# Two more table parts held, a shared tile for them and a pair of places, one uF tile, another cut of the last part, splits further ahead in two chunks

## The chip, the cores and the metric

One core of a Trainium2 chip runs the kernel. The metric is the device time of one execution in microseconds (us), from start to end. Durations of single instructions and transfers come from a profiled execution of the same program.

## The reference

The inputs are a table of 100,001 rows of 128 floats, 1024 sequences of 50 item numbers, and 1024 lengths. The reference gathers the rows, takes prefix means over the 50 steps, normalises each step over the batch, runs a spiking recurrence over the 50 steps, and multiplies the spike rates by the whole table:

```python
emb = emb_table.at[0].set(0.0)
e = emb[seq]                                   # 1024 x 50 x 128
uF = cumsum(e, axis=1) / minimum(t, lengths)   # prefix means
y = (uF - uF.mean(0)) * rsqrt(uF.var(0) + 1e-5) * gamma + beta
def step(v, x):
    v = v + (x - v) / 2.0
    spike = (v >= 1.0)
    return v - spike, spike
scores = spikes.mean(axis=0) @ emb.T           # 1024 x 100001, float32
```

The scores are 409.6 MB, and the table is 51.2 MB.

## The kernel before

**Two stages.** The first runs 50 steps. GpSimd (POOL) gathers eight times 128 table rows a step (`gather`, L196), TensorE (PE) transposes and accumulates them (L309, L270), VectorE (DVE) and ScalarE (ACT) do the statistics and the recurrence (L318 to L366). The second, from about 580 us on, computes the scores: counts (spike counts, 8 blocks of 128 batch rows) times the table.

**Parts, pairs, places.** The table is cut into 98 parts of 1024 rows; the last has 673. A part lies in SBUF as 128 partitions x 4 KB. `prepare` splits a part: eight PE transposes (L124) into a PSUM tile `pt`, an ACT copy that rounds to `hi` (L146), a DVE subtraction for the rest, `lo` (L147). A pair (hi, lo) needs a free place of 8 KB per partition; the list `free` hands places out first in, first out. `product` makes two matmuls for each 512 columns, so four per part and block (L154). Four PSUM tiles of 1024 columns serve products and transposes in turn.

**Chunks and blocks.** `WIDTHS` cuts the 98 parts into chunks: four of 2 parts (c = 0 to 3), four of 3 (c = 4 to 7), thirteen of 6 (c = 8 to 20). Within a chunk, n runs over the 8 batch blocks. A block (c, n) multiplies its parts, evicts them from PSUM into an output tile `o`, by DVE (L483) and ACT (L485) in turn, and stores the tile with one DMA on SP's queue (L163): 1 MB, 1.5 MB or 3 MB. `ready` issues one split after blocks n = 2 to 6, and one behind each part of block n = 7, if a place is free and the limit q2 (the end of the next chunk) isn't reached. The program order of each engine is the order in which this is written (`manual_schedule`).

**Where the parts come from.** 38 parts (`held`) are loaded on SP's queue in the first stage: six groups of six, and, when parts 0 and 1 have been split at t = 42 and 44, two more in their places. The other 60 come on ACT's queue in the second stage, three at a time, at n = 1 and 4 of the chunks from c = 8 on. The last of these loads takes two whole parts, the 673 rows' 640 first as 128 x 5 pieces of 512 B (L111), and 33 single rows (L116).

**Output tiles and where they lie.** Pools are laid out in the order in which they are opened, tiles within a pool in the order in which their tags are first used. Phase-one pools (`once`, ..., `uF`, `gather`) and later the pool `o` begin at the same address, behind the rows. In bytes per partition from that address:

| chunks | in the pool `o` | order of output tiles |
|---|---|---|
| 0 to 3 | third pair 0 to 8192; o0 from 8192, o1 from 16384, o2 from 24576, o3 from 32768, 8 KB each | o0, o1, o2, o3 |
| 4 to 7 | o2 from 0, o0 from 12288, o1 from 24576, 12 KB each | o2, o0, o1 |
| 8 to 20 | two pairs 0 to 16384; o 16384 to 40960 | the rows' tile 2, the rows' tile 3, o |

Chunks 4 to 7 have 32 blocks, so block (7, 5) uses o1, (7, 6) o2 and (7, 7) o0. The first two 1024-column results of block (0, 0) go out through single 4 KB tiles: one in a gather buffer, one in the second `uF` buffer, 23200 bytes from the start of the pool `once`. In that pool `rlen` lies at 7584 to 11680. A tile that is laid over older ones waits for the readers of each tile that it overlaps.

**Semaphores of the transfers.** The trace names a semaphore for each DMA. Those of SP's and ACT's queues together take eight of them in turn, and each issue first waits on the semaphore that it is going to use.

Of the kernel before, what the change touches and what calls it, by code (L numbers as in the profile page):

```python
# [12 lines left out]
F32 = mybir.dt.float32  # L13
BF16 = mybir.dt.bfloat16
F32R = mybir.dt.float32r
# [5 lines left out]
P = 128  # L21
BN_EPS = 1e-5
V_TH = 1.0
HALF = 1024
KQ = HALF // P
BANK = 512
GROUP = 6
AHEAD = 6
ONLY = 5
TWICE = 2  # L30

WIDTHS = 4 * [2] + 4 * [3] + 13 * [6]
NARROW, MIDDLE = 4, 8
# [3 lines left out]
def rec_kernel(  # L37
# [9 lines left out]
    nc = tc.nc  # L47
    B, T = seq.shape
    N, D = table.shape
    NB = B // P  # L50
# [8 lines left out]


    rowp = ctx.enter_context(tc.tile_pool(name="rows", bufs=1))


    countA = const.tile([P, P], F32R, tag="countA", name="countA")
# [5 lines left out]
    ident = const.tile([P, P], F32, tag="ident", name="ident")  # L70
# [2 lines left out]

    parts = -(-N // HALF)
    assert sum(WIDTHS) == parts
    held = AHEAD * GROUP + TWICE
    rows = {}
    split = {}

    free = []  # L80
# [4 lines left out]
    def size(q):  # L85
        return min(HALF, N - q * HALF)

    def group(g):
        at = g if g < AHEAD else AHEAD - 2 + g % 2
        r = rowp.tile([P, GROUP, HALF], F32, tag=f"rows{at}", name=f"rows_{g}")  # L90
        for k in range(GROUP):
            rows[g * GROUP + (TWICE if g else 0) + k] = r[:, k, :]
        return r

    def fetch(r, q, n):

        engine = nc.sync if q < held else nc.scalar
        k = q if q < GROUP else (q - TWICE) % GROUP
        n = min(n, parts - q)
        whole = n - (size(q + n - 1) < HALF)  # L100
        if whole:
            engine.dma_start(
                out=r[:, k : k + whole, :],
                in_=table[q * HALF : (q + whole) * HALF, :].rearrange("(q p k) d -> p q (k d)", p=P, k=KQ),
            )
        if whole < n:
            full, rest = divmod(size(parts - 1), P)
            c1 = (parts - 1) * HALF
            r = r[:, k + whole, :].rearrange("p (k d) -> p k d", d=D)
            if full:  # L110
                engine.dma_start(  # L111
                    out=r[:, :full, :],
                    in_=table[c1 : c1 + full * P, :].rearrange("(k p) d -> p k d", p=P),
                )
            if rest:
                engine.dma_start(out=r[:rest, full, :], in_=table[c1 + full * P : N, :])  # L116

    def turned(q, pt):
        r = rows.pop(q)
        if q == 0:  # L120
            nc.vector.memset(r[0:1, :D], 0.0)
        for k0 in range(0, size(q), P):
            kw = min(P, size(q) - k0)
            nc.tensor.transpose(pt[:, k0 : k0 + kw], r[:kw, k0 : k0 + D], ident[:kw, :kw])  # L124

    def views(q, pt, hi, lo):
        hw = size(q)
        if hw < HALF:
            return pt[:, :hw], hi[:, :hw], lo[:, :hw]
        return (  # L130
            pt.rearrange("d (k p) -> d p k", k=KQ),
            hi.rearrange("d (p k) -> d p k", k=KQ),
            lo.rearrange("d (p k) -> d p k", k=KQ),
        )


# [1 line left out]
    def prepare(q, pt):  # L138
        turned(q, pt)
        split[q] = hi, lo = free.pop(0)  # L140
        hw = size(q)
        if hw % 2:
            nc.vector.memset(hi[:, hw : hw + 1].bitcast(F32), 0.0)
            nc.vector.memset(lo[:, hw : hw + 1].bitcast(F32), 0.0)
        vp, vh, vl = views(q, pt, hi, lo)
        nc.scalar.copy(vh, vp)  # L146
        nc.vector.tensor_tensor(vl, vp, vh.bitcast(F32), ALU.subtract)  # L147
# [18 lines left out]
    with ExitStack() as ph:  # L166
        once = ph.enter_context(tc.tile_pool(name="once", bufs=1))
        lp = ph.enter_context(tc.tile_pool(name="lif", bufs=1))
        sp = ph.enter_context(tc.tile_pool(name="stats", bufs=3))
        up = ph.enter_context(tc.tile_pool(name="uF", bufs=2))  # L170
        gp = ph.enter_context(tc.tile_pool(name="gather", bufs=2))
        accp = ph.enter_context(tc.tile_pool(name="acc", bufs=1, space=bass.MemoryType.PSUM))
        vp = ph.enter_context(tc.tile_pool(name="v", bufs=1, space=bass.MemoryType.PSUM))
# [8 lines left out]
        nc.sync.dma_start(out=gb[:, 0:1], in_=gamma.rearrange("(d o) -> d o", o=1))  # L182
        nc.sync.dma_start(out=gb[:, 1:2], in_=beta.rearrange("(d o) -> d o", o=1))
        first = group(0)
        fetch(first, 0, GROUP)
        for g in range(1, AHEAD):
            fetch(group(g), g * GROUP + TWICE, GROUP)

# [42 lines left out]
        rlen = once.tile([P, B], F32, tag="rlen", name="rlen")  # L233
# [57 lines left out]
        whole = slice(0, B)  # L291
# [6 lines left out]
        for t in range(T):  # L298
            last = t == T - 1
            e = es.pop(t)  # L300
# [4 lines left out]
            uF = up.tile([P, B], F32, tag="uF", name=f"uF_{t}")  # L305
# [26 lines left out]
            r = sp.tile([P, 1], F32, tag="r", name=f"r_{t}")  # L332
# [14 lines left out]
            q = sp.tile([P, 1], F32, tag="q", name=f"q_{t}")  # L347
# [20 lines left out]
            if not last:  # L368
                vt = vp.tile([P, B], F32, tag=f"v{t % 2}", name=f"v_{t}")
                x(vt, whole)  # L370
                if t:
                    spiked(count, whole, v)
                step(vt, whole)
                v = vt
                d = over(t, v)
                if t + 2 < T:
                    l = only(t + 2)

                if t in (T - 8, T - 6):
                    q = (t - T + 8) // 2  # L380
                    pair(q)
                    prepare(q, vp.tile([P, HALF], F32, tag="v1", name=f"pt_{q}"))
                    if q == TWICE - 1:
                        for k in range(TWICE):
                            rows[GROUP + k] = first[:, k, :]
                        nc.sync.dma_start(
                            out=first[:, :TWICE, :],
                            in_=table[GROUP * HALF : (GROUP + TWICE) * HALF, :].rearrange(
                                "(q p k) d -> p q (k d)", p=P, k=KQ
                            ),  # L390
                        )
# [16 lines left out]

        po0 = accp.tile([P, HALF], F32, tag="po0", name="po_0_0")
        po1 = vp.tile([P, HALF], F32, tag="v0", name="po_0_1")  # L410
        for q, (pool, tag, po) in enumerate(((gp, "e", po0), (up, "uF", po1))):
            o = pool.tile([P, HALF], F32, tag=tag, name=f"o_0_{q}")
            for h, cs in enumerate(halves):
                product(po[:, cs], q, 0, h * BANK, BANK)
            for h, cs in enumerate(halves):
                if q and h:
                    nc.vector.tensor_scalar_mul(o[:, cs], po[:, cs], 1.0 / T)
                else:
                    nc.scalar.mul(o[:, cs], po[:, cs], 1.0 / T)
                store(0, q * HALF + h * BANK, o[:, cs])  # L420
# [10 lines left out]
    q0 = 0  # L431
    to_split = WIDTHS[0]
    to_fetch = held

    def places(at):
        t = rowp.tile([P, GROUP, HALF], F32R, tag=f"rows{at}", name=f"pairs_{at}")
# [2 lines left out]
    for c, W in enumerate(WIDTHS):  # L439

        if c in (0, NARROW, MIDDLE):
            opening.close()
            where = opening if c < MIDDLE else ctx
            op = where.enter_context(tc.tile_pool(name="o", bufs=1, reuse_waits="tile"))
            if c == 0:
                third = [op.tile([P, HALF], F32R, tag=x, name=x) for x in ("hi2", "lo2")]
                free.append(third)
                turns = [(op, f"o{k}", 2) for k in range(4)]
            elif c == NARROW:
                assert third in free  # L450
                free.remove(third)
                turns = [(op, f"o{k}", 3) for k in (2, 0, 1)]
            else:
                fourth = op.tile([P, 4, HALF], F32R, tag="pairs", name="pairs")
                free.extend((fourth[:, k, :], fourth[:, k + 1, :]) for k in (0, 2))
                turns = [(rowp, "rows2", 6), (rowp, "rows3", 6), (op, "o", 6)]
            blocks = 0
        q1 = q0 + W
        q2 = q1 + (WIDTHS[c + 1] if c + 1 < len(WIDTHS) else 0)

        def ready():
            nonlocal to_split
            if to_split < q2 and free:
                prepare(to_split, psum.tile([P, HALF], F32, tag="ps", name=f"pt_{to_split}"))
                to_split += 1

                if to_split in (GROUP + TWICE, 2 * GROUP + TWICE):
                    places(to_split // GROUP - 1)

        for n in range(NB):  # L470
            if c == 0 and n == 0:
                continue
            pool, tag, most = turns[blocks % len(turns)]
# [17 lines left out]
                    ready()  # L491
            if c or n > 1:
                store(n, q0 * HALF, o[:, : min(N, q1 * HALF) - q0 * HALF])
            if 2 <= n < NB - 1:
                ready()

            if n in (1, 4) and c >= MIDDLE and to_fetch < parts:
                g, k = divmod(to_fetch - TWICE, GROUP)
                if k or to_split >= (g - 1) * GROUP + TWICE:
                    if k == 0:  # L500
                        r = group(g)
                    fetch(r, to_fetch, GROUP // 2)
                    to_fetch += GROUP // 2
        assert to_split == q2
        q0 = q1


# [17 lines left out]
```

## Time and profile before

| what | value |
|---|---|
| median of 5 runs | 1642.88 us (1642.73 to 1648.5) |
| profiled execution, own time | 1643.19 us |
| its span, first to last instruction | 1641.1 us |
| PE / DVE / ACT / POOL busy | 1093.5 / 944.0 / 668.8 / 387.8 us |
| stores on SP's queue and the loads before them | 429.81 MB |
| loads on ACT's queue in the second stage | 31.28 MB |
| mean granted TensorE clock | 0.96 |

The page has the busy time of each engine, the span in 40 slices of 41 us (busy tenths, granted clock, DMA share, GB/s), the DMA queues, the chain of work that ended last, and the costliest groups. Other views of the trace are the waits by engine, the chain in order of time, the timeline, tables of stretches, and for each DMA the times at which its 16 shares landed. In a timeline line, the bracket says how long the engine stood idle before the instruction and what ended that.

### The profile page before, as it was taken

The numbers are of one execution on the slowest core, as the hardware profiler recorded it, in microseconds if no ns is written. First come the engines' busy times: TensorE is split into PE (matmuls) and PEld (weight loads), VectorE is DVE, ScalarE is ACT, GpSimd is POOL, SyncE is SP. The second block draws the span as 40 slices with busy tenths as digits, with TensorE's granted clock in tenths as the row PEclk, the third lists the DMA queues.
The fourth block names the chain that finished last, engine by engine and source line by source line (L and its number), as shares of the span: only waits on it lengthen the run. The fifth ranks groups of instructions, "written<-read, shape, count | busy, mean of one in ns | idle before, by whom it ended". The sixth has DMA issues, their size and how long they took to land.

```text
span 1641.1 us, 12239 instructions
## 1 busy us (share of the span) xinstructions
PE 1093.5 (67%) x4450; PEld 812.3 (50%) x4450; DVE 944.0 (58%) x1125; ACT 668.8 (41%) x697; POOL 387.8 (24%) x408
## 2 busy tenths in 40 slices
PE   4332333333333399888988788888788887888884
PEld 2111111111122276666866666666666666666763
DVE  5665665665565866566755555555545555555552
ACT  2332332332333355455544444444444444444442
POOL 7666666666766600000000000000000000000000
PEclk9999999999999999999999999899989999999998
DMA  9511111111111289999999999999999999999998
GB/s 349 209 47 45 48 47 47 45 46 46 49 48 45 64 328 416 405 424 414 405 425 427 431 431 422 419 427 421 424 430 417 419 418 415 431 427 419 398 430 342
DMA packets 51897, 488.12 MB, mean 297 GB/s; under 512 B 10075, under 2 KB 11004, under 8 KB 30588
## 3 DMA queue, kind: packets, MB, share of 16 engines
q1 hardware_dynamic: 30464, 429.81, 62.3%
q0 software_dynamic: 12800, 26.24, 5.5%
q10 hardware_dynamic: 8572, 31.28, 4.8%
q8 instruction: 35, 0.57, 0.1%
q14 instruction: 26, 0.21, 0.0%
HBM read 77.69 MB, written 409.60 MB: 297 GB/s over the span
## 4 chain that ended last, share of the span: by engine, by line
DMA 45%; POOL 13%; PE 12%; DVE 9%; issue 7%; another core or an unknown queue 7%; ACT 6%; ACTq 0%; SPq 0%; DVEq 0%; POOLq 0%
DMA scores<-o 44%; POOL e L196 13%; PE po L154 11%; ACT o L485 4%; DVE bs L319 2%; DVE uF L318 1%; DVE v L366 1%; DVE o L483 1%; DVE negv L286 1%; DMA e<-in_L_rec_emb_table,idx 1%; ACT v L363 1%; DVE count L289 1%; PE pt L124 0%; ACT pairs L146 0%
## 5 line engine op out<-in xcount | busy, mean ns | idle before, releaser
L483 DVE TENSOR_SCALAR o<-po 128x1024 f32<-128x1024 f32 x391 | 464.4, 1221 | 345.5 <-DMA scores<-o 305.1
L485 ACT ACTIVATE o<-po 128x1024 f32<-128x1024 f32 (+1 forms) x391 | 389.7, 1018 | 539.1 <-DMA scores<-o 320.1
L196 POOL DMA_INDIRECT e<-in_L_rec_emb_table,idx x400 | 382.2, 956 | 182.4 <-issue 106.6
L154 PE MATMUL po<-pairs,countB 128*128 128x512 f32 x1136 | 305.1, 414 | 60.9 <-ACT o L485 44.0
L154 PEld LDWEIGHTS po<-pairs,countB 128*128 128x128 f32 x1136 | 218.2, 197 | 123.9 <-ACT o L485 59.1
L154 PE MATMUL po<-pairs,countC 128*128 128x512 f32 x852 | 235.8, 423 | 46.6 <-ACT o L485 46.5
L270 PE MATMUL pre<-zT,ls 128*128 128x512 f32 x100 | 78.9, 791 | 270.3 <-DVE uF L318 213.4
L154 PEld LDWEIGHTS po<-pairs,countC 128*128 128x128 f32 x852 | 166.8, 202 | 92.5 <-ACT o L485 58.1
L270 PEld LDWEIGHTS pre<-zT,ls 128*128 128x128 f32 x100 | 29.2, 293 | 310.1 <-DVE uF L318 237.8
L309 PE MATMUL pre<-ident,e 128*128 128x128 f32 x400 | 127.0, 436 | 80.4 <-DMA e<-in_L_rec_emb_table,idx 54.9
L318 DVE SCALAR_TENSOR_TENSOR uF<-rlen,pre 128x512 f32<-128x512 f32 x100 | 68.0, 680 | 174.1 <-remote 156.0
L309 PEld LDWEIGHTS pre<-ident,e 128*128 128x128 f32 x400 | 80.4, 208 | 128.3 <-DMA e<-in_L_rec_emb_table,idx 84.0
L147 DVE TENSOR_TENSOR pairs<-pt,pairs 128x1024 fp32r<-128x1024 f32 x71 | 86.3, 1222 | 94.5 <-ACT pairs L146 94.3
L333 ACT ACTIVATE r<-mv,eps 128x1 f32<-128x1 f32 x50 | 14.7, 295 | 286.0 <-DVE mv L329 196.0
L124 PE MATMUL pt<-ident,rows 128*128 128x128 f32 x782 | 113.3, 293 | 8.7 <-issue 4.9
L124 PEld LDWEIGHTS pt<-ident,rows 128*128 128x128 f32 x782 | 103.1, 154 | 27.4 <-issue 13.1
L154 PE MATMUL po<-hi,countB 128*128 128x512 f32 x216 | 88.7, 411 | 18.3 <-ACT o L485 13.8
L154 PE MATMUL po<-lo,countB 128*128 128x512 f32 x216 | 86.5, 402 | 0.0
L282 ACT ACTIVATE d<-v,less 128x1024 bf16<-128x1024 f32 x49 | 54.5, 1113 | 63.5 <-DVE v L366 41.5
L154 PE MATMUL po<-hi,countC 128*128 128x512 f32 (+1 forms) x162 | 68.4, 422 | 15.1 <-ACT o L485 15.0
L146 ACT CAST pairs<-pt 128x1024 fp32r<-128x1024 f32 x71 | 71.8, 1012 | 15.8 <-PE pt L124 15.8
L154 PE MATMUL po<-pairs,countA 128*128 128x512 f32 x284 | 71.2, 394 | 8.5 <-ACT o L485 8.3
(78 smaller groups left out, 848.9 us busy)
## 6 DMA issues: line engine op xcount, KB each, us to landing
scores<-o SPq DMA_DIRECT2D x96, 3072.0 KB
scores<-o SPq DMA_DIRECT2D x32, 1536.0 KB
scores<-o SPq DMA_DIRECT2D x30, 1024.0 KB
rows<-in_L_rec_emb_table ACTq DMA_DIRECT2D x19, 1536.0 KB
scores<-o SPq DMA_DIRECT2D x8, 2896.5 KB
rows<-in_L_rec_emb_table SPq DMA_DIRECT2D x6, 3072.0 KB
e<-in_L_rec_emb_table,idx POOLq DMA_INDIRECT x400
rows<-in_L_rec_emb_table SPq DMA_DIRECT2D x1, 1024.0 KB
```

Of the source, the lines that this page charges most:

```text
L124: nc.tensor.transpose(pt[:, k0 : k0 + kw], r[:kw, k0 : k0 + D], ident[:kw, :kw])
L146: nc.scalar.copy(vh, vp)
L147: nc.vector.tensor_tensor(vl, vp, vh.bitcast(F32), ALU.subtract)
L154: nc.tensor.matmul(po[:, :kw], lhsT=counts[n], rhs=part[:, k0 : k0 + kw], start=j == 0, stop=j == 1,)
L196: nc.gpsimd.indirect_dma_start(out=es[t][:, n * P : (n + 1) * P], out_offset=None, in_=table, in_offset=bass.IndirectOffsetOnAxis(ap=idx[: ...
L270: nc.tensor.matmul(pre[h], lhsT=l, rhs=zT[:, h * BANK : (h + 1) * BANK], start=t == 0, stop=False, skip_group_check=True,)
L282: nc.scalar.activation(d, v, AF.Identity, bias=less)
L309: nc.tensor.matmul(pre[h][:, k : k + P], lhsT=e[:, h * BANK + k : h * BANK + k + P], rhs=ident, start=False, stop=last, is_transpose=True, ...
L318: nc.vector.scalar_tensor_tensor(uF[:, cs], rlen[:, cs], 1.0 / (t + 1), pre[h], ALU.max, ALU.mult)
L319: nc.vector.bn_stats(bs[:, h, :], uF[:, cs])
L483: nc.vector.tensor_scalar_mul(o[:, h0 : h0 + hw], po[:, :hw], 1.0 / T)
L485: nc.scalar.mul(o[:, h0 : h0 + hw], po[:, :hw], 1.0 / T)
```

## The change

Forty parts are held. A new pool `aside`, opened right behind the rows and before the first stage's pools, holds a tile of 8 KB with parts 2 and 3 (`spare`). Its loads come between those of parts 0, 1 and 4 to 7 of the first group. When parts 2 and 3 have been split, the tile becomes the third pair. The pool `aside` is closed before chunk 4. So the third pair is no longer in the pool `o` of chunks 0 to 3, and is not free from the start. The pool `uF` has one buffer; the second result of block (0, 0) goes through `rlen`'s place. The pools of the first stage, and the pool `o` of chunks 0 to 3, begin 8 KB further on.

The last part is laid out as the others: 84 rows of 4 KB in one DMA, and one piece of 512 B; rows 64 to 95 are first cleared by DVE. Its split takes eight transposes of 85 rows.

In chunks 5 and 6 the limit of `ready` is 1 and 2 parts higher, and in chunk 8 splits are issued from n = 0 on. The output tiles of chunks 8 to 20 come in the order o, tile 2, tile 3.

```diff
+ASIDE = 2
+SHIFT = TWICE + ASIDE
+FURTHER = {5: 1, 6: 2}
...
+    beside = ExitStack()
+    asidep = beside.enter_context(tc.tile_pool(name="aside", bufs=1))
...
-    held = AHEAD * GROUP + TWICE
+    held = AHEAD * GROUP + SHIFT
...
         if whole < n:
-            full, rest = divmod(size(parts - 1), P)
+            full, rest = divmod(size(parts - 1), KQ)
             c1 = (parts - 1) * HALF
-            r = r[:, k + whole, :].rearrange("p (k d) -> p k d", d=D)
+            r = r[:, k + whole, :]
+            if rest:
+                at = full - full % 32
+                nc.vector.memset(r[at : at + 32, :], 0.0)
+                engine.dma_start(
+                    out=r[full : full + 1, : rest * D],
+                    in_=table[c1 + full * KQ : N, :].rearrange("(o k) d -> o (k d)", o=1),
+                )
             if full:
                 engine.dma_start(
-                    out=r[:, :full, :],
-                    in_=table[c1 : c1 + full * P, :].rearrange("(k p) d -> p k d", p=P),
+                    out=r[:full, :],
+                    in_=table[c1 : c1 + full * KQ, :].rearrange("(p k) d -> p (k d)", k=KQ),
                 )
-            if rest:
-                engine.dma_start(out=r[:rest, full, :], in_=table[c1 + full * P : N, :])
...
-        up = ph.enter_context(tc.tile_pool(name="uF", bufs=2))
+        up = ph.enter_context(tc.tile_pool(name="uF", bufs=1))
...
-        fetch(first, 0, GROUP)
+        fetch(first, 0, 0, TWICE)
+        spare = asidep.tile([P, ASIDE, HALF], F32, tag="aside", name="spare")
+        for k in range(ASIDE):
+            rows[TWICE + k] = spare[:, k, :]
+        fetch(spare, 0, TWICE, ASIDE)
+        fetch(first, TWICE, SHIFT, GROUP - TWICE)
...
-        for q, (pool, tag, po) in enumerate(((gp, "e", po0), (up, "uF", po1))):
+        for q, (pool, tag, po) in enumerate(((gp, "e", po0), (once, "rlen", po1))):
...
             opening.close()
+            if c == NARROW:
+                assert third in free
+                free.remove(third)
+                beside.close()
...
-                third = [op.tile([P, HALF], F32R, tag=x, name=x) for x in ("hi2", "lo2")]
-                free.append(third)
                 turns = [(op, f"o{k}", 2) for k in range(4)]
...
-                turns = [(rowp, "rows2", 6), (rowp, "rows3", 6), (op, "o", 6)]
+                turns = [(op, "o", 6), (rowp, "rows2", 6), (rowp, "rows3", 6)]
...
-            if to_split < q2 and free:
+            if to_split < q2 + FURTHER.get(c, 0) and free:
                 prepare(...)
                 to_split += 1
-                if to_split in (GROUP + TWICE, 2 * GROUP + TWICE):
+                if to_split == SHIFT:
+                    t = asidep.tile([P, ASIDE, HALF], F32R, tag="aside", name="third")
+                    third = (t[:, 0, :], t[:, 1, :])
+                    free.append(third)
+                if to_split in (GROUP + SHIFT, 2 * GROUP + SHIFT):
                     places(to_split // GROUP - 1)
...
-            if 2 <= n < NB - 1:
+            if (2 if c != MIDDLE else 0) <= n < NB - 1:
                 ready()
```

More of the change, by code (lines that the diff above doesn't have):

```diff
@@ L86, in size, with deep @@
         return min(HALF, N - q * HALF)
+    def deep(q):
+        return -(-size(q) // KQ)
     def group(g):
@@ L91, in group, with fetch @@
         for k in range(GROUP):
-            rows[g * GROUP + (TWICE if g else 0) + k] = r[:, k, :]
+            rows[g * GROUP + SHIFT + k if g else k + ASIDE * (k >= TWICE)] = r[:, k, :]
         return r
-    def fetch(r, q, n):
+    def fetch(r, k, q, n):
         engine = nc.sync if q < held else nc.scalar
-        k = q if q < GROUP else (q - TWICE) % GROUP
         n = min(n, parts - q)
@@ L121, in turned @@
             nc.vector.memset(r[0:1, :D], 0.0)
-        for k0 in range(0, size(q), P):
-            kw = min(P, size(q) - k0)
-            nc.tensor.transpose(pt[:, k0 : k0 + kw], r[:kw, k0 : k0 + D], ident[:kw, :kw])
+        pw = deep(q)
+        for k0 in range(0, HALF, P):
+            nc.tensor.transpose(pt[:, k0 : k0 + pw], r[:pw, k0 : k0 + D], ident[:pw, :pw])
     def views(q, pt, hi, lo):
-        hw = size(q)
-        if hw < HALF:
-            return pt[:, :hw], hi[:, :hw], lo[:, :hw]
+        pw = deep(q)
         return (
-            pt.rearrange("d (k p) -> d p k", k=KQ),
-            hi.rearrange("d (p k) -> d p k", k=KQ),
-            lo.rearrange("d (p k) -> d p k", k=KQ),
+            pt.rearrange("d (k p) -> d p k", k=KQ)[:, :pw, :],
+            hi[:, : pw * KQ].rearrange("d (p k) -> d p k", k=KQ),
+            lo[:, : pw * KQ].rearrange("d (p k) -> d p k", k=KQ),
         )
@@ L140, in prepare @@
         split[q] = hi, lo = free.pop(0)
[L141 to L144, printed above, removed]
         vp, vh, vl = views(q, pt, hi, lo)
@@ L184, in rec_kernel @@
         first = group(0)
-        fetch(first, 0, GROUP)
+        fetch(first, 0, 0, TWICE)
[4 more added lines that the diff above has]
+        fetch(first, TWICE, SHIFT, GROUP - TWICE)
         for g in range(1, AHEAD):
-            fetch(group(g), g * GROUP + TWICE, GROUP)
+            fetch(group(g), 0, g * GROUP + SHIFT, GROUP)
         es = {}
@@ L384, in rec_kernel @@
                         for k in range(TWICE):
-                            rows[GROUP + k] = first[:, k, :]
+                            rows[GROUP + ASIDE + k] = first[:, k, :]
                         nc.sync.dma_start(
                             out=first[:, :TWICE, :],
-                            in_=table[GROUP * HALF : (GROUP + TWICE) * HALF, :].rearrange(
+                            in_=table[(GROUP + ASIDE) * HALF : (GROUP + SHIFT) * HALF, :].rearrange(
                                 "(q p k) d -> p q (k d)", p=P, k=KQ
@@ L433, in rec_kernel @@
     to_fetch = held
+    third = None
     def places(at):
@@ L445, in rec_kernel @@
             if c == 0:
-                third = [op.tile([P, HALF], F32R, tag=x, name=x) for x in ("hi2", "lo2")]
-                free.append(third)
                 turns = [(op, f"o{k}", 2) for k in range(4)]
             elif c == NARROW:
-                assert third in free
-                free.remove(third)
                 turns = [(op, f"o{k}", 3) for k in (2, 0, 1)]
@@ L461, in ready @@
         def ready():
-            nonlocal to_split
-            if to_split < q2 and free:
+            nonlocal to_split, third
+            if to_split < q2 + FURTHER.get(c, 0) and free:
                 prepare(to_split, psum.tile([P, HALF], F32, tag="ps", name=f"pt_{to_split}"))
                 to_split += 1
-                if to_split in (GROUP + TWICE, 2 * GROUP + TWICE):
+                if to_split == SHIFT:
[3 more added lines that the diff above has]
+                if to_split in (GROUP + SHIFT, 2 * GROUP + SHIFT):
                     places(to_split // GROUP - 1)
@@ L493, in rec_kernel @@
                 store(n, q0 * HALF, o[:, : min(N, q1 * HALF) - q0 * HALF])
-            if 2 <= n < NB - 1:
+            if (2 if c != MIDDLE else 0) <= n < NB - 1:
                 ready()
             if n in (1, 4) and c >= MIDDLE and to_fetch < parts:
-                g, k = divmod(to_fetch - TWICE, GROUP)
-                if k or to_split >= (g - 1) * GROUP + TWICE:
+                g, k = divmod(to_fetch - SHIFT, GROUP)
+                if k or to_split >= (g - 1) * GROUP + SHIFT:
                     if k == 0:
                         r = group(g)
-                    fetch(r, to_fetch, GROUP // 2)
+                    fetch(r, k, to_fetch, GROUP // 2)
                     to_fetch += GROUP // 2
-        assert to_split == q2
+        assert to_split >= q2
         q0 = q1
```

## The prediction

> **What bounds the kernel now.** I read the page first (slices, queues, chain), then the chain in order of time, the waits of SP's queue, the timeline where chunks change, and the landing times of the stores' 16 shares.
>
> ```profile
> DMA  9511111111111289999999999999999999999998
> q1 hardware_dynamic: 30464, 429.81, 62.3%
> q10 hardware_dynamic: 8572, 31.28, 4.8%
> DMA scores<-o 44%; POOL e L196 13%; PE po L154 11%; ACT o L485 4%; DVE bs L319 2%; DVE uF L318 1%; DVE v L366 1%; DVE o L483 1%; DVE negv L286 1%; DMA e<-in_L_rec_emb_table,idx 1%; ACT v L363 1%; DVE count L289 1%; PE pt L124 0%; ACT pairs L146 0%
> ```
>
> From slice 15 on the DMA engines are full: the second stage is bound by moving bytes, the first by POOL's gathers (13% of the chain, hardly any of them after 570 us). In the second stage time can be gained by fewer bytes or fewer idle DMA engines, and by nothing else. But which engine? The chain's last stretch:
>
> ```profile
> 1519.81 12.56 another core or an unknown queue
> ...
> 1532.80 3.30 another core or an unknown queue
> ...
> 1536.19 17.44 DMA scores<-o
> ...
> 1558.01 18.20 DMA scores<-o
> 1550.00:1575.00 25.00, 22.13 (x99) 17.78 (x98) 14.01 (x14) 11.84 (x13) 0.00 (x0) 0.93 1.00 426
> ```
>
> A DMA piece of the chain ends when a store's last share has landed: 1553.63 and 1576.21, three stores of 3.146 MB apart, 7.53 us each, or 418 GB/s. The window's mean over all engines is 426, and the first shares of the same stores land 7.3 us apart. So one share is 3% slower than the rest and falls behind: in the landing times the last trails the first by 1.5 us at 797 us and by 8.5 us at 1538. The slowest share's landings follow each other at 2.5, 3.85 and 7.55 us (1, 1.5 and 3 MB) through every change of chunk. It never waits: at the end of chunk 7 they are 785.80, 789.64, 797.17, although the other engines idled 2.7 us there. Its work sets the end. Idle time of the others is free while they lead; idle time that reaches the slowest share counts in full.
>
> **Two parts fewer to load in the second stage.** Between the landings at 842.54 and 1491.35 lie 77 stores and 59 whole parts: 648.8 - 77 x 7.55 = 67.5 us, 1.14 us a part on the slowest share. By the queue row (4.8% of 1641.1 us for 59.66 parts) it is 1.32. I take 2 x 1.14 = **-2.3** (to -2.6). The same 1 MB comes in the first stage instead. There the DMA engines are full until 62 us, and 1 MB at 390 GB/s makes that 64.7. POOL's gathers come 1.26 us apart under that load as after it, but its first long stop (4.9 us, before 59.68) lies under the load and could grow: **0**, at most +2.7.
>
> **The last part.**
>
> ```profile
> SPq L163 <- DMA rows<-in_L_rec_emb_table: 25.6, 3, 12.6
> ```
>
> Stores waited for loads of rows. The 512 B pieces issued at 1478.66 and 1479.99 landed at 1532.38 and 1536.10, and the stores that take their semaphores again, eight transfers later, could issue only at 1532.47 and 1536.19. The engines idled some 2.9 us (shares 0.73, 0.26 and 0.55 in the three 2-us windows from 1528). The slowest share, 8.5 us behind, felt little of it: 1538.00 to 1546.11 is 8.1 us instead of 7.55. So 84 rows of 4 KB, which land as early as other loads (28 us or less), are worth **-0.5**, not 2.9. The pieces themselves go from about 0.7 us on the slowest share to 0.8 (0.66 parts at 1.14), so the ends are -1.9 and +0.3. DVE's clear of 32 rows (a memset of 1024 elements took 0.91 us) and two more transposes (0.13 us each) lie in a stage whose stores are issued 17 to 20 us before they land, some 10 us more than their own transfer: 0. ACT's DMA waits for that clear, and ACT's evictions behind it: 1 to 2 us, under the same cover. [...]
>
> **One uF tile.** The last reader of a step's uF is ACT's L363; DVE's L366 waits for it (ends 568.98, starts 569.01), and only then DVE comes to the next L318 (570.15). The new wait is met by program order. At the start, isz's transposes end at 6.1 us and rb is written at 8.56; 2.4 us of cover. **0**.
>
> **The start of the scores.** The second result of block (0,0) now sits in rlen's place, 7584 bytes into a pool over which o0 (0 to 8192) is laid. So block (0,1) must wait for its store, which landed at 584.90. Before, it was block (0,2) that waited:
>
> ```profile
> 582.75 1.23 DVE L483 TENSOR_SCALAR o<-po 128x1024 f32<-128x1024 f32 x1 [0.34 <-PE po L154]
> 585.03 1.22 DVE L483 TENSOR_SCALAR o<-po 128x1024 f32<-128x1024 f32 x1 [1.06 <-DMA scores<-o]
> ```
>
> The first line moves to 585.0, the store behind it from 584.00 to 586.3. A store that finds idle engines starts 1.2 us after its issue (issued at 584.00, 0.5 MB landed at 586.49, of which 1.28 is transfer). The DMA stream then runs without a break: 1 MB to 590.0, block (0,2) to 592.5, (0,3) to 595.0, where its first share landed at 593.67: **+1.3**. Were the wait not there, the split no longer made at n = 2 would give back the 0.7 us of DMA idle near 590; with the eviction's full delay (585.03 - 582.75) it is +2.3.
>
> **Splits at other places.** Each costs 1.04 us on PE, 1.0 on ACT, 1.2 on DVE; their number stays. Parts 2 and 3 are now both split in block (0,7), just before they are needed. By these prices block (1,0) is stored at 602.3; the stores ahead of it end at 605, so 1.5 us are left after the 1.2 of start. Parts 9 and 10 are split in block (3,7). They are ready by 660.5, and the evictions that need them wait anyway until 661.96 (next fence). Both **0**; if the cover fails, what is beyond it counts. Chunks 5 and 6 have room (3 products at 0.92 and a split, 3.8 us, against 3.85 of DMA).
>
> **Chunk 8 starts in o.** What a tile laid over older ones waits for is seen where chunk 4 starts:
>
> ```profile
> 653.26 8.59 DMA scores<-o
> 661.96 1.02 ACT L485 ACTIVATE o<-po 128x1024 f32<-128x1024 f32 x1 [4.11 <-DMA scores<-o]
> 661.98 2.36 DVE L483 TENSOR_SCALAR o<-po 128x1024 f32<-128x1024 f32 x2 [3.91 <-DMA scores<-o]
> ```
>
> Block (4,0) goes to bytes 0 to 12288. Its first eviction writes 0 to 4096, and waits for the store of (3,5), from 8192 to 16384: whole tiles. Two stores were still queued behind that one, so nothing was lost. Now block (8,0) goes to o, 16384 to 40960, over (7,7)'s tile, 12288 to 24576. (7,7) is the last store issued: when it has landed nothing is queued. Both evicting engines stand in front of this wait, PE's four PSUM tiles fill, and nobody can store. Before, block (8,0) went to the rows' tile 2 and waited for nothing. From such a landing to the next issue, with four products ready:
>
> ```profile
> 1515.20 1.94 ACT L485 ACTIVATE o<-po 128x1024 f32<-128x1024 f32 x2 [3.41 <-DMA scores<-o]
> 1515.22 3.51 DVE L483 TENSOR_SCALAR o<-po 128x1024 f32<-128x1024 f32 x3 [4.15 <-DMA scores<-o]
> 1518.42 1.03 ACT L485 ACTIVATE o<-po 128x1024 f32<-128x1024 f32 x1 [1.28 <-PE po L154]
> ```
>
> The store landed at 1515.09, the next was issued at 1519.48: 4.4 us. With 1.2 of start the slowest share idles **+5.6**. Ends: 3.0 if half of the evictions were not held; 8.9 if the issue came 7.7 us after the landing (1561.18 to 1568.90). Afterwards blocks (8,1) and (8,2) each carry a split and are issued some 6.4 us apart (797.99, 804.34), against 7.55 of DMA: a lead of about 1 us, growing.
>
> **Sum.** -2.3 - 0.5 + 1.3 + 5.6 = +4.1: 1643.19 + 4.1 = 1647.3 for the profiled execution, and, as the median lies 0.3 below it, **1647.0**. What a measurement can tell from no change is 0.2%, 3.3 us: 1639.6 to 1646.2.
>
> **Rivals.** *The start of chunk 8 is covered* (0.2): the wait is by bytes in another way than I read, or falls away. For it: the kernel has such waits hidden at chunk 4. Against: there two stores were queued, here none. It decides at 1.5 us of idle: with less, the other terms make the time no slower. With none it is 1647.0 - 5.6 = 1641.4, not slower. *All DMA engines count alike* (0.1): then the gap near 1530 is worth 2.9, two parts 2.6, and of chunk 8's idle the 2.7 of before are deducted, while the faster engines wait 1 us longer: -2.6 - 2.9 + 1.3 + 3.9 = -0.3, 1642.6. Against it: the last shares' even pace over 765 to 797 us. *The first stage gets longer* (0.1): the 1 MB delays POOL by its full 2.7: 1649.7. Against it: the even pace of the gathers under load. That the change doesn't do what it says, I exclude: 58 parts are left to load, and in chunks 5 and 6 places are free for 4 splits each.
>
> **How the numbers follow.** My forecast has 0.6, on its own 1645 to 1649. Slower by over 0.2%: 0.55 of these 0.6 and the 0.1 of the longer first stage, 0.65. Within: the rest of the 0.6, most of the two rivals, 0.27. Faster: their lower edges (the last part at its -1.9, no cost at the start), 0.08. The range takes in the first rival and the longer first stage: 1641.0 to 1649.7.
>
> **What would show it.** Right: at the start of chunk 8 (some 790 us) both DVE and ACT wait for a store at L483 and L485, and the DMA share is near 0 for over 5 us; DVE's first L483 is at 585; no SP wait for rows after 1400; end of the first stage as before, at 580.7. Wrong: no gap near 790, or a first store of scores more than 1 us later than 580.74, or a slowest share that idles elsewhere.

## The result and the profile after

The changed kernel takes 1650.98 us in the median of 22 runs, the kernel before 1643.00 in 42 runs beside it. The ratio is 1.0048 (95% interval 1.0039 to 1.0057): slower by 8.0 us in the medians, where 4.0 were forecast (1647.0, range 1641.0 to 1649.7). The direction was right; the size was not, and the median lies 1.3 us above the range.

The profiled execution of after took 1647.44 us (span 1645.3; before 1643.19 and 1641.1). These two profiles differ by 4.25 us, near the forecast's 4.1, and that is luck: this execution is quicker than each of the 22 runs, and its first store comes 2.5 us earlier than in before. The lines of its page that answer to those of before:

```profile
DMA  9611111111112189999799999999999999999997
GB/s 351 230 46 47 46 47 46 49 48 46 46 46 71 38 354 416 404 422 406 326 429 425 430 431 425 428 424 424 423 427 419 411 422 424 427 419 415 427 415 336
q10 hardware_dynamic: 7700, 30.23, 4.6%
```

Slice 19 (781 to 823 us) has a 7 where before had a 9, and 326 GB/s: the stop that the prediction placed near 790. The queue of the second stage's loads (q10) carries 1.05 MB less, the two parts. The timeline there (start, duration, engine, what, and in brackets the idle time before it with what ended it):

```profile
788.81 1.94 ACT L501 ACTIVATE o<-po 128x1024 f32<-128x1024 f32 x2 [8.52 <-DMA scores<-o]
788.85 2.35 DVE L499 TENSOR_SCALAR o<-po 128x1024 f32<-128x1024 f32 x2 [7.10 <-DMA scores<-o]
789.89 3.78 PE L160 MATMUL po<-pairs,countA 128*128 128x512 f32 x8 [6.52 <-ACT o L501]
793.70 1.02 ACT L501 ACTIVATE o<-po 128x1024 f32<-128x1024 f32 x1 [2.95 <-PE po L160]
794.75 0.33 SPq L169 DMA_DIRECT2D scores<-o  x1
```

Both evicting engines wait for the store of (7,7), whose last share landed at 788.63. The next store is issued at 794.75, 6.1 us later, and lands at 803.47, 14.84 us after the one before it instead of 7.53. So the slowest share idles 7.3 us; 5.6 were forecast. The same place in windows of 2 us (busy time and count of PE, PEld (its weight loads), DVE, ACT, POOL, then PE's granted clock, DMA share, GB/s):

```profile
784.00:786.00 2.00, 0.00 (x0) 0.00 (x0) 0.00 (x0) 0.00 (x0) 0.00 (x0) 1.00 1.10 461
786.00:788.00 2.00, 0.00 (x0) 0.00 (x0) 0.00 (x0) 0.00 (x0) 0.00 (x0) 0.80 0.12 49
788.00:790.00 2.00, 0.11 (x1) 0.11 (x1) 1.15 (x2) 1.19 (x2) 0.00 (x0) 0.50 0.00 0
790.00:792.00 2.00, 2.00 (x5) 1.61 (x6) 1.21 (x3) 0.75 (x1) 0.00 (x0) 0.50 0.01 4
792.00:794.00 2.00, 2.00 (x7) 1.51 (x7) 1.22 (x1) 0.30 (x1) 0.00 (x0) 0.50 0.00 0
794.00:796.00 2.00, 2.00 (x13) 1.75 (x12) 0.13 (x1) 1.75 (x2) 0.00 (x0) 0.99 0.46 197
```

PE had four products ready and stood idle from 783.4 to 789.9. Its granted clock was 0.50 when the fifth and sixth product came: eight matmuls in 3.78 us.

At the start of the scores, DVE's first L499 waits for the store of (0,0), as forecast:

```profile
582.53 3.67 DVE L499 TENSOR_SCALAR o<-po 128x1024 f32<-128x1024 f32 x3 [2.61 <-DMA scores<-o]
```

And no store waits for rows any more after 1400 us (waits of SP's queue: total, times, longest; L537 is the end of the kernel):

```profile
SPq L169 <- DVE o L499: 201.1, 29, 11.1
SPq L169 <- ACT o L501: 17.7, 22, 1.5
SPq L537 <- DMA scores<-o: 9.4, 2, 6.8
```

The first store of scores was issued at 578.25, before at 580.74. As the first experiment shows, this moment varies between runs by more than that.

### The profile page after: what moved, and what is told of

The parts are those of the page before. It is cut to its first block, busy times and chain, and to the rows that moved or that the text cites. A ratio compares the mean times of both kernels' runs of the same rounds, so it can differ in the third digit from the quotient of the medians.

```text
span 1645.3 us, 12233 instructions
## 1 busy us (share of the span) xinstructions
PE 1090.5 (66%) x4452; PEld 805.7 (49%) x4452; DVE 943.1 (57%) x1124; ACT 668.0 (41%) x697; POOL 389.4 (24%) x408
## 3 DMA queue, kind: packets, MB, share of 16 engines
q1 hardware_dynamic: 30752, 430.86, 62.3%
## 4 chain that ended last, share of the span: by engine, by line
DMA 47%; DVE 13%; PE 11%; POOL 9%; another core or an unknown queue 7%; ACT 6%; issue 5%; ACTq 0%; DVEq 0%; SPq 0%; POOLq 0%
DMA scores<-o 46%; PE po L160 10%; POOL e L207 9%; ACT o L501 5%; DVE bs L330 3%; DVE uF L329 2%; DVE v L377 2%; DVE negv L297 2%; DVE o L499 1%; ACT v L374 1%; DVE count L300 1%; DMA e<-in_L_rec_emb_table,idx 1%; DVE a L370 0%; DVE mv L340 0%
## 5 line engine op out<-in xcount | busy, mean ns | idle before, releaser
L499 DVE TENSOR_SCALAR o<-po 128x1024 f32<-128x1024 f32 x391 | 464.2, 1221 | 352.2 <-DMA scores<-o 316.4
L501 ACT ACTIVATE o<-po 128x1024 f32<-128x1024 f32 (+1 forms) x391 | 389.2, 1019 | 550.2 <-DMA scores<-o 337.6
L160 PE MATMUL po<-pairs,countB 128*128 128x512 f32 (+1 forms) x1120 | 295.2, 410 | 64.8 <-ACT o L501 49.9
L160 PEld LDWEIGHTS po<-pairs,countB 128*128 128x128 f32 x1120 | 212.6, 195 | 127.7 <-ACT o L501 66.7
L160 PE MATMUL po<-pairs,countC 128*128 128x512 f32 (+1 forms) x840 | 230.4, 421 | 47.6 <-ACT o L501 47.3
L136 PE MATMUL pt<-ident,rows 128*128 128x128 f32 (+1 forms) x768 | 108.7, 288 | 10.0 <-issue 4.9
L136 PEld LDWEIGHTS pt<-ident,rows 128*128 128x128 f32 (+1 forms) x768 | 98.5, 152 | 28.1 <-issue 12.8
L160 PE MATMUL po<-hi,countC 128*128 128x512 f32 x156 | 65.7, 421 | 14.8 <-ACT o L501 14.7
```

Of the source, the lines that this page charges most:

```text
L136: nc.tensor.transpose(pt[:, k0 : k0 + pw], r[:pw, k0 : k0 + D], ident[:pw, :pw])
L160: nc.tensor.matmul(po[:, :kw], lhsT=counts[n], rhs=part[:, k0 : k0 + kw], start=j == 0, stop=j == 1,)
L499: nc.vector.tensor_scalar_mul(o[:, h0 : h0 + hw], po[:, :hw], 1.0 / T)
L501: nc.scalar.mul(o[:, h0 : h0 + hw], po[:, :hw], 1.0 / T)
```

## The experiments

They ran on several chips; each is compared with the kernel before on its own chip.

| run | median us | kernel before | ratio (95%) |
|---|---|---|---|
| e1 after again | 1586.13 | 1579.80 | 1.0041 (1.0025 to 1.0056) |
| e2 tile 2 first | 1579.13 | 1579.80 | 0.9997 (0.9987 to 1.0006) |
| e3 before, o first | 1587.12 | 1579.80 | 1.0045 (1.0032 to 1.0059) |
| e4 gather place | 1584.26 | 1579.80 | 1.0029 (1.0018 to 1.0040) |
| e5 both places | 1639.86 | 1642.53 | 0.9985 (0.9970 to 1.0001) |
| e6 before, last cut | 1642.28 | 1642.53 | 0.9998 (0.9981 to 1.0015) |
| e9 PE kept busy | 1646.66 | 1642.53 | 1.0028 (1.0011 to 1.0045) |
| e10 after, third time | 1649.20 | 1642.53 | 1.0041 (1.0025 to 1.0057) |
| e11 both places again | 1640.17 | 1642.87 | 0.9982 (0.9971 to 0.9994) |
| e12 both places, old last cut | 1639.39 | 1642.87 | 0.9980 (0.9968 to 0.9993) |

**e1: the changed kernel again**, no edit.

> The changed kernel once more, unchanged, for a second profile beside the first. Theory (the slowest of the 16 DMA shares sets the end; idle time that reaches it counts in full): some 7 to 8 us slower than the kernel before in the median; the gap of about 15 us between the landings of the last store of chunk 7 and the first of chunk 8 comes back within 2 us (near 788 to 803 us), with 6 us from landing to issue and a granted clock of 0.5 for the last part of PE's idle time. If the first stage is longer in this kernel (the rival with 1 MB more at the start), its first store of scores comes at 582 to 583 instead of 580.7; if the first profile's 578.25 is chance, it may fall anywhere from 578 to 583.

Measured: 6.3 us slower than the kernel before. Chunk 8's first store landed 14.84 us after the last of chunk 7, issued 6.1 us after that landing, as in the first profile. But everything is 63 us shorter, for the kernel before too. Its first stage ends at 517.00, and POOL's group of gathers shows why. Of the profile of before, and of e1:

```profile
L196 POOL DMA_INDIRECT e<-in_L_rec_emb_table,idx x400 | 382.2, 956 | 182.4 <-issue 106.6 <-remote 62.3 <-DMA e<-in_L_rec_emb_table,idx 7.0
```
```profile
L207 POOL DMA_INDIRECT e<-in_L_rec_emb_table,idx x400 | 382.5, 956 | 123.8 <-issue 117.6 <-DMA idx<-in_r_seq 2.2 <-PE pre L320 2.1
```

On this chip POOL has none of the long stops (14 with a "remote" releaser, up to 5.5 us, in the profile of before) that lengthen the first stage on the other chips; what causes them is not known. So here the change can be read without them. The kernel before's own first stage ends at 516.97 (in e3's profile, which shares it); the changed one's at 516.58 to 517.00 (e1, e2, e4): within this spread of 0.4 us the first stage costs nothing. On a chip with stops their places differ from run to run, and with them the end of the stage: 578.25 to 581.57 in six profiles with the change's first stage, 580.74 for before, 584.12 in e6.

**e2: tile 2 first in the changed kernel.**

```diff
-                turns = [(op, "o", 6), (rowp, "rows2", 6), (rowp, "rows3", 6)]
+                turns = [(rowp, "rows2", 6), (op, "o", 6), (rowp, "rows3", 6)]
```

> The changed kernel, with block (8,0) in the rows' tile 2 again and (8,1) in o, so nothing waits for the last store of chunk 7. Theory: the 7.3 us of idle DMA near 790 us go, the slowest share goes on at 7.55 us a store, and the time falls by 7.3 us against the changed kernel, to 1643.5 or so, within 1 us of the kernel before. By the term of the prediction (5.6) it falls by 5.6 only. Rival (the wait was covered, and the time lost lies elsewhere, in the first stage): less than 2 us. Rival (all DMA engines count alike): 7.3 - 2.7 = 4.6 us.

Measured: 7.0 us less than e1, where the forecast's term says 5.6 and the rival of equal engines 4.6. The first store of chunk 8 lands 7.52 us after the last of chunk 7. Its windows at the same place:

```profile
726.00:728.00 2.00, 2.00 (x10) 1.34 (x8) 1.42 (x2) 0.66 (x1) 0.00 (x0) 1.00 0.95 399
728.00:730.00 2.00, 1.64 (x8) 1.32 (x8) 2.00 (x3) 1.28 (x2) 0.00 (x0) 1.00 0.92 393
```

The clock is full, and the DMA share is 0.95 and 0.92 around the last landing of chunk 7 (727.16). Turning this one line back gives back all that the change loses: the 0.7 us by which e2 is below the kernel before lie inside the interval.

**e3: the same order in the kernel before.**

```diff
-                turns = [(rowp, "rows2", 6), (rowp, "rows3", 6), (op, "o", 6)]
+                turns = [(op, "o", 6), (rowp, "rows2", 6), (rowp, "rows3", 6)]
```

> The kernel before with only the order of the three tiles from chunk 8 on turned to o, tile 2, tile 3. Theory: 5.6 (the prediction's term) to 7.3 us slower than the kernel before, with a gap between the landings at the end of chunk 7 of 13 to 15 us instead of 7.5; the clock of PE falls to 0.5 after some 3.5 us of idle. Rival (covered): within 1 us of the kernel before. Rival (all DMA engines alike): 7.3 - 2.7 = 4.6 us.

Measured: 7.3 us slower than the kernel before, 14.74 us between the landings. The loss needs nothing else of the change. PE's clock fell 2.2 us into its pause, not after some 3.5 (3.8 in after). In both directions the idle time of the slowest share counts in full (7.0 us in e2 for 7.3, 7.3 here for 7.2), though before the other 15 shares idled 2.7 us there: that idle time of theirs was worth nothing that shows.

**e4: another place for the second result of block (0,0).**

```diff
-        for q, (pool, tag, po) in enumerate(((gp, "e", po0), (once, "rlen", po1))):
+        for q, (pool, tag, po) in enumerate(((gp, "e", po0), (gp, "e", po1))):
```

> The changed kernel, with the second result of block (0,0) in the second buffer of the gathers instead of rlen's place, so that no tile of the second stage that is used at once lies over it. Theory: DVE's first eviction of the second stage no longer waits for a store (its group at 582.5 has PE as what ended its wait), and the time falls by 1.3 to 1.4 us. Rival (the 1.3 is covered, because the slowest share starts its first stores no earlier): 0. Nothing changes near 790 us.

Measured: 1.9 us less than e1; 1.4 expected. DVE's first L499 waits for nothing; ACT's first L501 still waits for a store:

```profile
518.90 1.21 DVE L499 TENSOR_SCALAR o<-po 128x1024 f32<-128x1024 f32 x1
520.33 1.03 ACT L501 ACTIVATE o<-po 128x1024 f32<-128x1024 f32 x1 [2.06 <-DMA scores<-o]
```

From the first store's issue to the last landing of chunk 7 it is 209.43 us in e3 (the start of before), 210.62 in e1, 208.64 in e4. Over all profiles it is 208.91 to 209.49 with the start of before (before, e3, e6), 210.38 to 210.63 with the change's (after, e1, e2, e9, e10), 208.23 to 209.00 with e4's (e4, e5, e11, e12). So the wait costs the change 1.2 us net by the means. What e4 wins beyond that, 0.7 to 0.8 against the start of before, has the size of the 0.7 of DMA idle that the split left out at n = 2 was to give back; that this is its cause is argued, no run changes that split alone.

**e5 and e11: both places moved**, the edits of e2 and e4 together, on two chips.

> The changed kernel with both places moved: block (8,0) in the rows' tile 2, and the second result of block (0,0) in the second gather buffer. Theory: the two idle times of the slowest share (7.3 and 1.9 us by the runs) add, so the time is 9.2 us less than the changed kernel's and 2.5 us less than the kernel before's (ratio 0.9984), with 841 us from the first landing of chunk 8 to the end, against 843. Rival (all DMA engines alike): the two are not independent of how far the slowest share lags, and less than 7 us is gained. Rival (first stage longer with the 1 MB more): the first store of scores comes over 1 us later than that of the kernel before.

> The kernel with both places moved, once more, to narrow the ratio to the kernel before (0.9985, from 0.9970 to 1.0001). Theory: -2.1 us from chunk 8 to the end and -0.4 to -0.8 us at the start of the scores, 2.5 to 2.9 us faster than the kernel before on every chip; ratio 0.9982 to 0.9985 with 1.0 outside the interval where POOL has no long stops.

Measured: 2.7 us faster than the kernel before both times, with 1.0 just inside the interval the first time and outside it the second. From chunk 8's first landing to the landing of the last store ("the end" below) it is 840.55 us in both profiles, against 842.85 in before. Against e10, on e5's chip, 9.3 us are gained; 9.2 were expected.

**e6: the new cut of the last part alone**, in the kernel before.

```diff
-            full, rest = divmod(size(parts - 1), P)
+            full, rest = divmod(size(parts - 1), KQ)
...
-                    out=r[:, :full, :],
-                    in_=table[c1 : c1 + full * P, :].rearrange("(k p) d -> p k d", p=P),
+                    out=r[:full, :],
+                    in_=table[c1 : c1 + full * KQ, :].rearrange("(p k) d -> p (k d)", k=KQ),
```

> The kernel before with only the last, partial part loaded as 84 rows of 4 KB and 1 row of 2 KB (with the clear of 32 rows and eight transposes). Theory (slowest share): the stores' waits for rows after 1400 us go, the faster shares no longer idle there, and the slowest share gains 0.5 us: 0.5 us faster, within what can be measured. Rival (all DMA engines alike): the 2.9 us of idle engines come back, 2.9 us faster. If the 32 rows' clear or the transposes cost anything: slower.

Measured: 0.3 us less, an interval of some 3 us on either side. Inconclusive by itself: 0, 0.5 and 2.9 fit. Its profile has no gain: 844.0 us from chunk 8's first landing to the end, 1.2 more than before and 1.0 more than e3. Nor does the cut alone take the waits away: the 84 rows landed 23.5 us after their issue here (11.0 to 12.6 in the profiles with the whole change), and one wait of 12.9 us is still put down to rows.

**e9: PE kept busy while chunk 8 waits**, in the changed kernel. The fourth product of block (8,0) is computed seven times.

```diff
-                for k0 in range(0, hw, BANK):
+                again = 7 if c == MIDDLE and n == 0 and q == q0 + 3 else 1
+                for k0 in again * list(range(0, hw, BANK)):
```

> The changed kernel, in which the fourth product of block (8,0) is computed seven times over into the same tile (six times for nothing), so that PE works while the evictions wait for the store of (7,7). Theory (the 1.7 us by which chunk 8's start was underestimated are PE's low clock after its idle time): the granted clock stays near 1, the next store is issued 4.3 us after the landing instead of 6.1, and the time falls by 1.8 us against the changed kernel. Rival (the 6.1 us are the evictions and the order of the products alone): no change, or slower by the end of the repeated products.

Measured: 2.5 us less than e10 on the same chip in the medians, 1.3 by the landings (13.17 us apart against 14.49; 14.84 in the first profile and e1). The chunk's start, where (7,7) has landed at 790.11:

```profile
783.68 6.51 PE L160 MATMUL po<-pairs,countA 128*128 128x512 f32 x28
790.29 1.94 ACT L502 ACTIVATE o<-po 128x1024 f32<-128x1024 f32 x2 [8.63 <-PE po L160]
791.37 2.12 PE L160 MATMUL po<-pairs,countA 128*128 128x512 f32 x8 [1.18 <-ACT o L502]
793.53 1.03 ACT L502 ACTIVATE o<-po 128x1024 f32<-128x1024 f32 x1 [1.29 <-PE po L160]
794.58 0.33 SPq L169 DMA_DIRECT2D scores<-o  x1
```

And the window of that kernel in which the eight matmuls begin:

```profile
790.00:792.00 2.00, 0.82 (x4) 0.55 (x4) 1.67 (x2) 1.71 (x2) 0.00 (x0) 1.00 0.01 4
```

The same eight matmuls take 2.12 us instead of 3.78, the clock stays at 1.00, and the store is issued 4.5 us after the landing. The slowest share idles 13.17 - 7.53 = 5.6 us, the figure of the forecast. What it lacked was PE's clock. Useless work that keeps PE's clock up made the changed kernel faster; it is still 4.1 us slower than the kernel before.

**e10: the changed kernel, third profile**, no edit.

> The changed kernel unchanged, as the reference for the other runs on the same chip, and for a third profile. Theory: 6.3 us slower than the kernel before where POOL has no long stops in the first stage (the first store of scores near 517 us), of which 7.3 are chunk 8's start; where it has such stops (first store near 580), the same sum, plus or minus what the stops differ from run to run (a few us).

Measured: 6.7 us slower than the kernel before, the mechanism's size again on a chip with POOL's stops. The landings are 14.49 us apart instead of 14.84: the eight matmuls begin at 791.21, the clock is back at 794.1, and they take 3.42 us instead of 3.78.

**e12: both places moved, the last part cut as before.**

```diff
-            full, rest = divmod(size(parts - 1), KQ)
+            full, rest = divmod(size(parts - 1), P)
```

(and the loads, transposes and views that go with it, as in the kernel before)

> The kernel with both places moved, but with the last part loaded as the kernel before does it (five rows of 512 B a partition, and 33 rows of 512 B). Tells the two parts held from the new cut within the 2.1 us gained after chunk 8's start. Prediction's terms: 0.5 us slower than with the new cut, so 2.3 for the two parts. If the cut is worth nothing (it gave 0.3 us by itself, within the error): the same time, and the two parts are the whole 2.1, 1.05 a part. If the waits of stores for rows after 1400 us came to bear in full (all DMA engines alike): 2.9 us slower.

Measured: the same as e11 (1639.39 against 1640.17, within what the runs can tell; 840.45 against 840.55 us from chunk 8 to the end). Its 512 B loads were issued at 1514.66 and 1515.07 and landed at 1553.01 and 1556.84, after 38.4 and 41.8 us (before: 53.7 and 56.1). The stores that take their semaphores again were issued behind that, at 1554.52 and 1563.96, and the queue shows no wait for rows after 1400 us:

```profile
SPq L170 <- DVE o L500: 194.1, 28, 9.5
SPq L170 <- ACT o L502: 16.5, 21, 1.5
SPq L538 <- DMA scores<-o: 16.3, 3, 6.9
```

The new cut is worth nothing here that the runs could tell, and the gain is that of holding two parts more, with what this does to the place of the last loads.

## Why the prediction was right in direction and wrong in size

| term | forecast | measured |
|---|---|---|
| two parts fewer | -2.3 | -2.1 (843.00 in e3 to 840.86 in e1), with o not first -2.3 (842.85 in before to 840.55 in e5); the end of the waits for rows is in it |
| last part | -0.5 | 0 for the new cut (e12 against e11) |
| first stage, one uF tile | 0 | 0 within 0.4 (516.58 to 517.00 against 516.97) |
| start of the scores | +1.3 | +1.2 (210.62 against 209.43) |
| chunk 8 in `o` | +5.6 | +7.3 (14.84 - 7.53) |
| sum | +4.1 | +6.4 |

**The step that failed is the price of chunk 8's start.** The mechanism, the place, the waiting engines and the idle DMA were as told; e2 and e3 show the wait by taking it away and by making it alone. The size was taken from the landing at 1515.09, because there too four products were ready. But PE's idle time before it was 1.92 us, its clock stayed at 1.00, and in this case PE idles 6.5 us:

```profile
1516.00:1518.00 2.00, 1.73 (x8) 1.42 (x8) 2.00 (x3) 1.14 (x2) 0.00 (x0) 1.00 1.04 445
```

The number of products ready was the wrong thing to match. The profile of before had the right row, at the landing of 1561.18, which I had used as the upper end:

```profile
1562.36 3.60 PE L154 MATMUL po<-pairs,countC 128*128 128x512 f32 x8 [2.01 <-ACT o L485]
```

and its window:

```profile
1562.00:1564.00 2.00, 1.64 (x4) 1.35 (x5) 2.00 (x5) 0.93 (x2) 0.00 (x0) 0.55 0.92 393
```

Eight matmuls in 3.60 us, at half the clock. With this row for the fifth and sixth product the term would have been 5.6 + 3.60 - 1.99 = 7.2 us, and the forecast 1648.6. In the stop of 6.5 us PE has been idle since 783.4, and the windows show 0.80 at 786 to 788, 0.50 until 794, and 0.99 thereafter: the clock fell at 787.2, 3.8 us into the pause, and was full again at 794.04, 4.15 us after the matmuls had begun. Before 1562.36 a pause of 2.01 us was enough. e9 tests the step: with PE at work, the eight matmuls take 2.12 us, the clock stays at 1.00, and the idle time is the forecast's 5.6 us.

**The last part's -0.5 fell too.** Its place in the profile was right (the waits for rows near 1530) and so was the warning that the slowest share felt little of it; without the waits and with two parts fewer it gains 2.1 to 2.3 us together, less than the -2.3 of the parts and the -0.5. That the new cut would end the waits was wrong as a reason: with it alone (e6) one wait stayed, and without it (e12) there was none. In e12 the pieces land 38 to 42 us after their issue and hold up nobody, so the form of the loads alone does not make the wait. In before a load of 1 MB was issued on the same queue 0.4 us ahead of them, in e12 the one ahead came 41 us earlier; whether that decides was not tried. The 84 rows land in fewer shares: in each of the eight profiles of the changed kernel that have the new cut, one event of that load comes within 1 us of its issue, and 14 landings 9 us after it or later, where the loads of three whole parts in after have 16 landings each. That this spares the slowest share is not seen: 840.55 us with the new cut, 840.45 with the old. And the other loads, which I took to land within 28 us, took 27.8 to 30.5 in before; no term rests on it.

**The rivals.** That chunk 8's start is covered is excluded by e2 and e3 (7.0 and 7.3 us, not 0). That all DMA engines count alike asked for 4.6 us in both; what was measured is the full idle time of the slowest share. Behind chunk 8's first landing it asked for 2.6 and 2.9 us, and 2.1 to 2.3 were gained in all, with the waits near 1530 gone. That the first stage gets longer by 2.7 us is excluded where POOL has no stops, and with them none of six profiles with the change's first stage shows it (at most 581.57 against 580.74).

**What is left.** The terms give +6.4, and the runs +6.3 (e1) and +6.7 (e10). The first comparison had +8.0. The intervals of the ratio overlap, so I take the rest for the first stage's spread with POOL's stops. With the mis-sized term put right the forecast would still be some 2 us short of the 1650.98; for that part the cause stays open. In e6's profiled run (1648.28 us, among 1640.4 to 1644.0 for most of its runs) DVE waited 7.15 us at the start of the stage's last step (4.96 in before), and the first store came at 584.12:

```profile
567.41 0.69 DVE L320 SCALAR_TENSOR_TENSOR uF<-rlen,pre 128x512 f32<-128x512 f32 x1 [7.15 <-remote]
```

That such a late step makes the longest runs of every kernel is argued from this one profile, not shown, and whether the changed kernel meets it more often stays open: 7 of its first 22 runs took 1655 us or more, but of the 12 in e10 only 2 took over 1654 (the others at most 1649.7), and of the kernel before 5 of 35 on that chip took over 1649 (the median 1642.5).

## What to carry to other kernels

Where a tile is laid over older ones, ask which store is the last issued before it is first written: if that one lies under it, put another tile first, since one line of order cost 7.3 us here and gave back all of it. When a stall is priced by a row of the trace, match the row by how long each engine behind it has stood idle, and read the granted clock beside it, not only by the work that is ready. And before idle transfer engines are counted as a gain, look whether the slowest of them was idle too.

## What the runs showed of the hardware

- PE's granted clock halved here after pauses far shorter than the 6.5 us at chunk 8's start: in before, 2.01 us before 1562.36 (0.55) and 1.89 us before 1523.90 (0.50, below) were enough, 1.92 us before 1516.28 was not (1.00). So the length of a pause alone did not decide. Into the same pause of 6.5 us the clock fell after 2.2 us (e3), 2.6 (e10), 3.5 (e1), 3.8 (after) or 5.3 (e4). In the clock's records of before, from 1400 to 1600 us, each of the seven falls (1408.61 the first, 1586.10 the last) comes at the end of 3.41 us in which PE worked 1.3 to 1.6 us, and lasts 3.41 us; the 3.41 us before 1516.28 held 1.5 us of work too, and no fall came. A pause of 6.5 us made the next eight matmuls 3.42 (e10) to 3.78 us (after) long instead of 2.12 (e9).

```profile
1526.00:1528.00 2.00, 2.00 (x9) 1.70 (x8) 0.62 (x1) 0.90 (x1) 0.00 (x0) 0.50 1.01 432
```

- The same kernel takes 1579.80 us on one chip and 1642.53 or 1642.87 on two others (whether the chip itself makes it was not tried). What differs is the first stage, whose end comes at 516.97 instead of 580.74 us with POOL's stops gone (62.3 us in the profile of before, none in e1 to e4); the store stage takes the same: 840.86 us from chunk 8's first landing to the end in e1 and in e10.
- Idle time of the faster DMA shares near 790 us (2.7) cost nothing, and that near 1530 (2.9) nothing that shows beside the loads of two parts; idle time of the slowest counted in full (7.0 and 7.3 us for 7.3 and 7.2). At the end of chunk 7 fifteen shares of a store land within 0.2 us, and one 1.5 to 2.1 us behind them.
